# A decoder block on one core: the second composed weight by seven block products, the first one's scaling on ScalarE

## The chip, the core and the metric

The kernel runs on one core of a Trainium2 chip. The metric is the device time of one execution in microseconds, the median of several runs. The engines are named as in the profile: PE is TensorE's matrix multiply and PEld its weight load, DVE is VectorE, ACT is ScalarE, POOL is GpSimd, SP is SyncE, which only issues DMAs. All data are f32, and an f32 matmul leaves two records in the trace.

## What is computed

`x` is (8, 256, 256): 8 sequences of 256 tokens with 256 features. Three blocks follow one another, each with a residual and a layer norm behind it.

- Four layers of attention (8 heads of 32; four local ones with a causal window of 128, four linear ones over buckets of 64), each followed by an MLP 256 to 1024 to 256 with exact gelu.
- A cross attention to a context of 120 tokens.
- A feed-forward block whose two weights are first composed:

```python
def _compose_weight(logits, A, B):        # A (64, d_in, 64), B (64, 64, d_out)
    vals, idx = top_k(logits, 32)
    w = softmax(vals)
    return einsum('k,kir,kro->io', w, A[idx], B[idx])
W1 = _compose_weight(fc1_logits, fc1_A, fc1_B)   # 256 x 1024
W2 = _compose_weight(fc2_logits, fc2_A, fc2_B)   # 1024 x 256
h = gelu(x @ W1);  y = h @ W2
```

The change lies in the composition. Each weight is a sum of 32 weighted products of rank 64. Two of them side by side have rank 128, which is one pass of TensorE's rows; so there are 16 pairs per weight.

## The kernel before, in words

**Order.** Lines 1100 to 1109 put PE, ACT, DVE and POOL under a manual schedule: each engine runs its instructions in the order in which the Python code calls them. The main loop (L1173) has 32 steps, one per layer and sequence. A step runs the attention of one sequence split in pieces (`old`, `new`, `after` are three sequences at different points), an MLP four steps behind (`ff`), and a piece of the composition. A second loop (L1283) does the cross attention and the feed-forward block.

**The composition.** The 16 pairs of a weight are taken in 8 groups of `PG` = 2; `n` is 0 for the first weight and 1 for the second, `g` the group. A group passes through these stages, each a method:

- `Group.__init__` (L325): six indirect DMAs from POOL's queue (L302), four for the rows of A (`ga`) and two for the rows of B (`gbt`).
- `weigh` (L341): VectorE multiplies the A rows by their softmax weights (L350), four instructions per group, 128x128 each for n = 0 and 128x512 for n = 1.
- `turns` (L359): TensorE transposes the weighted A (L369), VectorE and ScalarE copy it from PSUM to `at` (L372 for n = 0, L377 and L379 for n = 1).
- `block(i)`, i from 0 to 3 (L382): TensorE multiplies `at` and the B rows into one PSUM bank; VectorE adds the bank to the running sum in `w2c` (L420 for the first group, L422 after; for n = 0 the last group goes to `w1c`, L400). For n = 0 a block is two matmuls of 512 columns (L387), for n = 1 four of 256 columns (L410).

`Compose.run` (L448) ties the stages together: `weigh` of the next group if that has not been done, the four blocks of the current group, `gather` of the group after the next, `turns` of the next. It is called three times in step 1, twice in steps 2 and 3, and once in each of steps 4 to 12 (L1184, L1221, L1247); the second weight's blocks run in steps 5 to 12. In steps with an MLP, `weigh` is called earlier (L1219). `filled` is true as long as the composition has not ended.

**Around it in a step.** Before `run` at L1247 stand: `new.exps` (L670: exponentials L672 and L673, then L685 for heads 0 and 1), `ff.second(1)` (matmuls L561 into the bank `ps_p`), `after.turn` (transposes L213 of the next sequence, evicted by VectorE at L222 and ScalarE at L223), the exponentials of heads 2 and 3, and `softmax_q` (L696 to L700). After `run` stand `totals` and `divide` (L709 to L715), `nxt_m.centre` (L195, and two bias adds on POOL, L230), `ff.second(0)` (L561, then the add L234 that empties `ps_p`), and the next step's `after.moments` (L181 to L189), `new.qkv` (L602, L622, evicted at L611 and L629 to L642), `linear_sums`, `divide_c` (L751 to L757), `turn_p` (L767, copies L770 and L772), `turn_sums` (L490 to L493 on POOL) and `scores` (L653).

**PSUM.** Two pools of four banks: `bank_s` for scores and projections, `bank_g` for the rest, the composition among it. `ps_p` holds one of the four from `second(1)` to `second(0)`.

**Seven products elsewhere.** The MLP's first matmul already goes by seven block products in place of eight (`first_sums` L472, class `Seven` L482, `one` L509 with its matmuls at L512): sums of blocks are formed on POOL (L476 to L479, 128x512, and L490 to L493, 128x128), and each product is four matmuls of 128 columns.

Of the kernel before, what the change touches and what calls it, by code (L numbers as in the profile page):

```python
# [8 lines left out]
F32 = mybir.dt.float32  # L9
I32 = mybir.dt.int32  # L10
AF = mybir.ActivationFunctionType
ALU = mybir.AluOpType
# [3 lines left out]
P = 128  # L16
# [5 lines left out]
def tile_decoder_postln(  # L22
# [46 lines left out]
    NP, _, R = fc1_A.shape  # L69
    TOPK = 32  # L70
    NPAIR = TOPK // 2
# [51 lines left out]
    w1c = const.tile([P, NC, FF], F32, name="w1c")  # L123
    w2c = const.tile([P, NF, D], F32, name="w2c")
# [46 lines left out]
    def bank_g(name):  # L171
        return ps_g.tile([P, 512], F32, tag="bank_g", name=name)
# [34 lines left out]
    def turn(src, tag, name, gain=None, shift=None):  # L207

        dst = work.tile([P, NC, T], F32, tag=tag, name=f"xT_{name}")
        ps = bank_g(f"ps_t_{name}")  # L210
        for c in range(NC):
            for i in range(WT):
                nc.tensor.transpose(  # L213
                    ps[:, c * T + i * P : c * T + (i + 1) * P],
                    src[:, i, c * P : (c + 1) * P],
                    ident,
                )
        if gain is None:
# [3 lines left out]
        nc.vector.tensor_scalar(dst[:, 0, :], ps[:, :T], gain(0), shift(0), ALU.mult, ALU.add)  # L222
# [29 lines left out]
    comp = comp_stack.enter_context(tc.tile_pool(name="comp", bufs=1))  # L252
# [59 lines left out]
    PG = 2  # L312
# [11 lines left out]
    class Group:  # L324
# [16 lines left out]
        def weigh(self):  # L341

            n, g, n_c = self.n, self.g, tables[self.n][2]
            wts = tops[n][2]
            self.aw = []
            for k, a in enumerate(self.a):
                t = g * PG + k
                aw = comp.tile([P, n_c, 2, R], F32, tag="aw", name=f"aw{n}_{t}", bufs=2)
                for e in range(2):
                    nc.vector.tensor_scalar(  # L350
                        aw[:, :, e, :],
                        a[:, e, :].rearrange("p (c r) -> p c r", c=n_c),
                        wts[:, 2 * t + e : 2 * t + e + 1],
                        None,
                        ALU.mult,
                    )
                self.aw.append(aw.rearrange("p c e r -> p c (e r)"))

        def turns(self):  # L359
            n, n_c = self.n, tables[self.n][2]  # L360
            self.at = []
            for k, aw in enumerate(self.aw):
                name = f"{n}_{self.g}_{k}"
                at_ = comp.tile([P, n_c * P], F32, tag="at", name=f"at{name}", bufs=4)
                for q in range(0, n_c, 4):
                    ps = bank_g(f"ps_at{name}_{q}")
                    m = min(4, n_c)
                    for c in range(m):
                        nc.tensor.transpose(ps[:, c * P : (c + 1) * P], aw[:, q + c, :], ident)  # L369
# [12 lines left out]
        def block(self, i):  # L382
            ps = bank_g(f"ps_w{self.n}_{self.g}_{i}")
            if self.n == 0:
                m, n = divmod(i, 2)
                for k in range(PG):
                    nc.tensor.matmul(  # L387
                        ps,
                        self.at[k][:, m * P : (m + 1) * P],
                        self.b[k][:, n * 512 : (n + 1) * 512],  # L390
                        start=k == 0,
                        stop=k == PG - 1,
                    )

                dst = w2c.rearrange("p f d -> p (f d)").rearrange("p (m o) -> p m o", m=NC)
                dst = dst[:, m, n * 512 : (n + 1) * 512]
                src = ps
                if self.g == NPAIR // PG - 1:
                    final = w1c[:, m, :].rearrange("q (j p) -> q p j", j=NF)
                    nc.vector.tensor_add(  # L400
                        final[:, n * 64 : (n + 1) * 64, :],
                        dst.rearrange("q (p j) -> q p j", j=NF),
                        src.rearrange("q (p j) -> q p j", j=NF),
                    )
                    return
            else:
                for e in range(2):
                    j = 2 * i + e
                    for k in range(PG):
                        nc.tensor.matmul(  # L410
                            ps[:, e * D : (e + 1) * D],
                            self.at[k][:, j * P : (j + 1) * P],
                            self.b[k],
                            start=k == 0,
                            stop=k == PG - 1,
                        )
                dst = w2c[:, 2 * i : 2 * i + 2, :].rearrange("p j d -> p (j d)")
                src = ps
            if self.g == 0:
                nc.vector.tensor_copy(dst, src)  # L420
            else:
                nc.vector.tensor_add(dst, dst, src)  # L422

    class Compose:

# [17 lines left out]
        def turn(self):  # L443
            self.turned, self.weighed = self.weighed, None
            if self.turned:
                self.turned.turns()

        def run(self):  # L448
            if self.turned is None:
                return  # L450
            if not self.weighed:
                self.weigh()
            for i in range(4):
                self.turned.block(i)
            self.gather()
            self.turn()

# [24 lines left out]
    class Seven:  # L482
# [26 lines left out]
        def one(self, n, ps, start=False, stop=False):  # L509

            for f in range(4):
                nc.tensor.matmul(  # L512
                    ps[:, f * P : (f + 1) * P],
                    self.ws[n][:, f * P : (f + 1) * P],
                    self.rhs[n],
                    start=start and f == 0,
                    stop=stop and f == 3,
                    skip_group_check=True,
                )
# [50 lines left out]
    class Attention:  # L570
# [99 lines left out]
        def exps(self):  # L670
            name = self.name
            nc.scalar.activation(self.qs, self.qs, AF.Exp)  # L672
            nc.scalar.activation(self.ke, self.ke, AF.Exp)  # L673
            self.p = []

            self.psum = small.tile([P, HL, 3], F32, tag="psum", name=f"psum_{name}")
            self.head_exps(range(2))

        def head_exps(self, heads):
            for h in heads:  # L680
# [173 lines left out]
    class Composed(Seven):  # L854
# [21 lines left out]
        def turn(self):  # L876
            self.xT = turn(xs[self.b], "xTm", self.name)
# [14 lines left out]
    class Context:  # L892
# [222 lines left out]
    new = Attention(0)  # L1115
    first = {n: top_k(n) for n in range(2)}
# [43 lines left out]
    compose.gather()  # L1160
    new.scores()
    new.exps()
    new.head_exps((2, 3))
    new.softmax_q()
    new.totals()
    new.divide(range(HL))
# [1 line left out]
    old, new = new, after  # L1168
# [4 lines left out]
    for s in range(1, UNITS + 1):  # L1173
# [3 lines left out]
        filled = cross is None  # L1177
# [55 lines left out]
        if turn_cx:  # L1233
            i = 2 * (s - (UNITS - B + LAG))
            cx.turn(i)
            cx.take()
        if new:
            new.exps()
        if ff:
            ff.second(1)  # L1240
        if after:
            after.turn()
        if new:
            new.head_exps((2, 3))
            new.softmax_q()
        if filled:
            compose.run()  # L1247
# [31 lines left out]
        old, new = new, after  # L1279
# [109 lines left out]
```

## Time and profile before

| | |
|---|---|
| median of 3 runs | 1248.43 us (1246.93 to 1251.41) |
| the profiled execution | 1256.8 us, its span 1254.9 us |
| mean granted clock of TensorE | 0.99 |
| from one group of the second weight to the next | 34.8 to 35.0 us |

Busy time in us, by stage of the span:

| stage | span | PE | DVE | ACT | POOL |
|---|---|---|---|---|---|
| 0 to 157 us, start and first weight | 157.0 | 132.8 | 113.0 | 48.3 | 78.2 |
| 157 to 192 us, last group of the first weight | 34.9 | 34.6 | 26.1 | 18.1 | 11.8 |
| 192 to 443 us, the second weight's eight groups | 250.9 | 250.9 | 177.2 | 133.0 | 85.4 |
| 443 us to the end | 812.1 | 803.7 | 531.5 | 429.3 | 207.3 |

In a row of the timeline stand the start, the time from first start to last end, the engine, the line, the operation, output and inputs, the shape and the number of instructions; in brackets the idle time before it and the instruction that ended it. Rows of one line without a gap are merged. A matmul's end is modelled, so pace is read from starts.

### The profile page before, as it was taken

To read this page: it belongs to the slowest core of one execution; us is meant where nothing else is said; L and a number is where in the kernel's file an instruction comes from. 1 tells how busy PE (TensorE), PEld (TensorE's weight loads), DVE (VectorE), ACT (ScalarE), POOL (GpSimd) and SP (SyncE) were. 2 spreads that over 40 slices of the span, in tenths; PEclk is the share of its full clock that TensorE was granted. 3 is DMA by queue.
4 is the path that set the end of the run, shared out by engine and by line. 5 is a ranking of instruction groups with operands and counts; after the bars stand their busy time and mean duration, and the time that the engine had idled before them with its cause. 6 is when DMAs were issued, how large, how long until landed. Compare 5 with 4: busy or idle time off the path is not lost.

```text
span 1254.9 us, 23452 instructions
## 1 busy us (share of the span) xinstructions
PE 1222.0 (97%) x8905; PEld 969.1 (77%) x8905; DVE 847.8 (68%) x2435; ACT 628.7 (50%) x1738; POOL 382.7 (31%) x596
## 2 busy tenths in 40 slices
PE   5999999999999999999999999999999999999998
PEld 3555678888888888888878888788888777777787
DVE  5787877767767667777777776777765454556543
ACT  2222544555555556667766677566773334233322
POOL 5445433333334111222322221242213323222210
PEclk8998999999999999999999999999999999999999
DMA  4532212111120021002001000120000000000000
GB/s 131 168 91 83 81 51 81 43 43 43 65 73 20 1 84 39 2 2 72 1 1 39 2 1 17 57 69 1 26 10 10 9 9 9 18 17 9 9 14 22
DMA packets 29502, 47.77 MB, mean 38 GB/s; under 512 B 3150, under 2 KB 22734, under 8 KB 29134
## 3 DMA queue, kind: packets, MB, share of 16 engines
q0 software_dynamic: 6656, 20.98, 5.6%
q10 hardware_dynamic: 13024, 14.07, 3.4%
q1 hardware_dynamic: 9710, 11.23, 2.8%
q8 instruction: 70, 1.15, 0.4%
q14 instruction: 42, 0.34, 0.1%
HBM read 44.17 MB, written 2.10 MB: 37 GB/s over the span
## 4 chain that ended last, share of the span: by engine, by line
PE 92%; DVE 3%; ACT 2%; POOL 1%; issue 1%; another core or an unknown queue 0%; DMA 0%; POOLq 0%; ACTq 0%; DVEq 0%
PE ps_p_m L561 17%; PE qkv_a L622 8%; PE ps_h_m_u L512 7%; PE ps_h_m_a L512 5%; PE ps_w L387 4%; PE ps_w L410 4%; PE ps_h_m_d L512 4%; PE ps_p_a L240 4%; PE ps_qk_a L602 4%; PE ps_p_f L561 4%; PE ps_pT_a L767 3%; PE sc_a L653 3%; PE ps_y_c L1085 2%; PE ps_xq_c L996 2%; PE ps_xk_c L996 2%; PE ps_xv_c L996 2%
## 5 line engine op out<-in xcount | busy, mean ns | idle before, releaser
L561 PE MATMUL ps_p_m<-w,h_m 128*128 128x256 f32 x1024 | 231.5, 379 | 0.0
L561 PEld LDWEIGHTS ps_p_m<-w,h_m 128*128 128x128 f32 x1024 | 189.8, 190 | 23.5 <-ACT h_m L827 0.3
L622 PE MATMUL qkv_a<-wa,xT_a 128*128 128x512 f32 x256 | 115.7, 595 | 0.0
L230 POOL TENSOR_TENSOR x<-x,b 128x256 f32<-128x256 f32 x64 | 48.2, 773 | 209.5 <-DVE xn_m L195 209.4
L685 ACT ACTIVATE p_a<-sc_a,nm_a 128x128 f32<-128x128 f32 (+1 forms) x256 | 103.9, 426 | 1.9 <-DVE nm_a L666 1.7
L622 PEld LDWEIGHTS qkv_a<-wa,xT_a 128*128 128x128 f32 x256 | 49.1, 192 | 48.1 <-issue 46.3
L230 POOL TENSOR_TENSOR x<-x,bo 128x256 f32<-128x256 f32 x64 | 48.2, 772 | 118.4 <-DVE xn_a L195 113.6
L666 DVE TENSOR_REDUCE nm_a<-sc_a 128x1 f32<-128x128 f32 (+1 forms) x256 | 79.7, 353 | 4.4
L827 ACT ACTIVATE h_m<-h_m,cols 128x128 f32<-128x128 f32 x256 | 78.6, 405 | 6.2 <-DVE h_m L549 5.5
L512 PE MATMUL ps_h_m_a<-xT_m,w 128*128 128x128 f32 x512 | 71.4, 283 | 0.0
L302 POOL DMA_INDIRECT ga<-in_L_ffn_fc_A_dram,idx_a x64 | 62.1, 971 | 21.2 <-issue 16.6
L512 PE MATMUL ps_h_m_u<-tx_m,w 128*128 128x128 f32 x512 | 67.6, 275 | 0.0
L629 ACT COPY v<-qkv_a 128x256 f32<-128x256 f32 x64 | 23.8, 372 | 86.3 <-PE qkv_a L622 85.0
L602 PE MATMUL ps_qk_a<-xT_a,wa 128*128 128x256 f32 x256 | 64.0, 395 | 2.8 <-DVE nm_a L666 2.1
L512 PEld LDWEIGHTS ps_h_m_a<-xT_m,w 128*128 128x128 f32 x512 | 63.2, 194 | 4.2 <-issue 1.6
L240 PE MATMUL ps_p_a<-wo,oT_a 128*128 128x256 f32 x256 | 65.4, 380 | 0.0
L662 DVE TENSOR_TENSOR sc_a<-sc_a,causal 128x256 f32<-128x256 f32 x128 | 54.5, 425 | 15.5 <-PE sc_a L653 15.5
L715 DVE TENSOR_TENSOR p_a<-p_a,psum_a 128x384 f32<-128x384 f32 x128 | 62.9, 553 | 1.1
L512 PEld LDWEIGHTS ps_h_m_u<-tx_m,w 128*128 128x128 f32 x512 | 62.3, 192 | 0.0
L602 PEld LDWEIGHTS ps_qk_a<-xT_a,wa 128*128 128x128 f32 x256 | 50.4, 199 | 11.1 <-ACT p_a L685 2.8
L561 PE MATMUL ps_p_f<-w2c,h_f 128*128 128x256 f32 x256 | 57.8, 379 | 0.0
L767 PE MATMUL ps_pT_a<-ident,p_a 128*128 128x128 f32 x384 | 52.3, 278 | 5.6 <-ACT pT_a L772 5.0
(245 smaller groups left out, 2655.2 us busy)
## 6 DMA issues: line engine op xcount, KB each, us to landing
w<-in_L_attn_W_dram ACTq DMA_DIRECT2D x8, 1024.0 KB, 7.6
xwkv<-in_L_xattn_Wkv_dram SPq DMA_DIRECT2D x1, 2048.0 KB
x_c<-in_x_dram SPq DMA_DIRECT2D x8, 256.0 KB, 2.7
out_dram<-y_f SPq DMA_DIRECT2D x16, 128.0 KB, 1.7
x<-in_x_dram ACTq DMA_DIRECT2D x6, 256.0 KB, 2.7
ga<-in_L_ffn_fc_A_dram,idx_a POOLq DMA_INDIRECT x64
xwq<-in_L_xattn_Wq_dram SPq DMA_DIRECT2D x1, 1024.0 KB
xwo<-in_L_xattn_Wout_dram SPq DMA_DIRECT2D x1, 1024.0 KB
```

The costliest lines, as they stand in the source:

```text
L230: nc.gpsimd.tensor_add(xb[:, i, :], xb[:, i, :], bias)
L240: nc.tensor.matmul(ps[:, i * D : (i + 1) * D], lhs(c, i), w[:, c, :], start=c == 0, stop=c == n_in - 1,)
L512: nc.tensor.matmul(ps[:, f * P : (f + 1) * P], self.ws[n][:, f * P : (f + 1) * P], self.rhs[n], start=start and f == 0, stop=stop and f == ...
L561: nc.tensor.matmul(self.ps[:, i * D : (i + 1) * D], self.h[k][:, f, :], self.w2[:, half * 4 + f, :], start=k in (11, 22) and f == 0, stop= ...
L602: nc.tensor.matmul(ps[:, s * T : (s + 1) * T], wa[:, c, s * HW : (s + 1) * HW], xT[:, c, :], start=c == 0, stop=c == NC - 1,)
L622: nc.tensor.matmul(t, xT[:, c, w * P : (w + 1) * P], wa[:, c, 2 * HW :], start=c == 0, stop=c == NC - 1,)
L666: nc.vector.tensor_reduce(self.nmax[:, h, w : w + 1], sc[:, s], AX.X, ALU.max, negate=True)
L685: nc.scalar.activation(flat[:, s], sc[:, s], AF.Exp, bias=self.nmax[:, h, w : w + 1], accum_out=self.psum[:, h, w : w + 1],)
L715: nc.vector.tensor_tensor(p, p, self.psum[:, h, :, None].to_broadcast([P, 3, P]), ALU.mult)
L767: nc.tensor.transpose(pp[:, k * P : (k + 1) * P], p[:, k, :], ident)
L827: nc.scalar.activation(dst[:, f, :], src[:, f * P : (f + 1) * P], AF.Gelu, bias=col("ff", i))
L996: nc.tensor.matmul(ps[:S2], lhs(c), w[:, c, off : off + 512], start=c == 0, stop=c == NC - 1)
```

## The change

For the second weight (n = 1) a group's 1024 x 128 by 128 x 256 products, two of them summed, are seen as a 2 x 2 block product: the blocks of A are two halves of `at` (512 columns) by the two pairs, those of B the two pairs by two halves of 128 columns. Eight block products become seven. `combine` forms eight sums on POOL, four of 128x128 and four of 128x512, two of them in place; it is called behind `turns`. `seven` makes the products on four banks and adds them to five running sums on VectorE: the four quarters of `w2c` and a tile `u` that three of the quarters share; after the last group POOL adds `u` to those three. Further: `weigh` for n = 0 goes to ScalarE, `at` has two buffers for four, and while the composition lasts all four head exponentials stand behind `after.turn` (the first two stood before it). `block` serves only n = 0 now, with the same instructions.

```diff
                 for e in range(2):
-                    nc.vector.tensor_scalar(
...
+                    if n == 0:
+                        nc.scalar.mul(dst, src, w)
+                    else:
+                        nc.vector.tensor_scalar(dst, src, w, None, ALU.mult)
...
-                at_ = comp.tile([P, n_c * P], F32, tag="at", name=f"at{name}", bufs=4)
+                at_ = comp.tile([P, n_c * P], F32, tag="at", name=f"at{name}", bufs=2)
...
-                for e in range(2):
-                    j = 2 * i + e
-                    for k in range(PG):
-                        nc.tensor.matmul(
-                            ps[:, e * D : (e + 1) * D],
-                            self.at[k][:, j * P : (j + 1) * P],
-                            self.b[k],
-                            start=k == 0,
-                            stop=k == PG - 1,
-                        )
-                dst = w2c[:, 2 * i : 2 * i + 2, :].rearrange("p j d -> p (j d)")
...
+        def combine(self):
+
+            a = [[at_[:, m * 512 : (m + 1) * 512] for at_ in self.at] for m in range(2)]
+            b = [[b_[:, n * P : (n + 1) * P] for n in range(2)] for b_ in self.b]
+            name = f"{self.n}_{self.g}"
+            s1, s2, s4 = (
+                comp.tile([P, 512], F32, tag=f"cs{i}", name=f"cs{i}_{name}") for i in (1, 2, 4)
+            )
+            t1, t2, t4 = (
+                comp.tile([P, P], F32, tag=tag, name=f"ct_{tag}_{name}") for tag in ("lb", "pb", "t4")
+            )
+            nc.gpsimd.tensor_sub(t1, b[0][1], b[0][0])
+            nc.gpsimd.tensor_sub(t2, b[1][1], t1)
+            nc.gpsimd.tensor_sub(t4, b[1][0], t2)
+            nc.gpsimd.tensor_sub(b[0][1], b[1][1], b[0][1])
+            nc.gpsimd.tensor_add(s1, a[1][0], a[1][1])
+            nc.gpsimd.tensor_sub(s2, s1, a[0][0])
+            nc.gpsimd.tensor_sub(s4, a[0][1], s2)
+            nc.gpsimd.tensor_sub(a[1][0], a[0][0], a[1][0])
+            self.factors = {
+                1: (a[0][0], b[0][0]),
+                2: (a[0][1], b[1][0]),
+                3: (s4, b[1][1]),
+                4: (a[1][1], t4),
+                5: (s1, t1),
+                6: (s2, t2),
+                7: (a[1][0], b[0][1]),
+            }
+
+        def one(self, i, ps, start=False, stop=False):
+            a, b = self.factors[i]
+            for f in range(4):
+                nc.tensor.matmul(
+                    ps[:, f * P : (f + 1) * P],
+                    a[:, f * P : (f + 1) * P],
+                    b,
+                    start=start and f == 0,
+                    stop=stop and f == 3,
+                    skip_group_check=True,
+                )
+
+        def seven(self):
+            c = [[w2c[:, 4 * m : 4 * m + 4, n * P : (n + 1) * P] for n in range(2)] for m in range(2)]
+            u = comp.tile([P, 4, P], F32, name="csum_u") if self.g == 0 else Group.u
+            Group.u = u
+
+            def take(dst, ps, first=False):
+                src = ps.rearrange("p (f i) -> p f i", f=4)
+                if self.g == 0 and first:
+                    nc.vector.tensor_copy(dst, src)
+                else:
+                    nc.vector.tensor_add(dst, dst, src)
+
+            name = f"ps_w{self.n}_{self.g}"
+            p6 = bank_g(f"{name}_6")
+            self.one(6, p6, True, True)
+            take(u, p6, True)
+            p12 = bank_g(f"{name}_12")
+            self.one(1, p12, start=True)
+            take(u, p12)
+            p53 = bank_g(f"{name}_53")
+            self.one(5, p53, start=True)
+            take(c[1][1], p53, True)
+            p74 = bank_g(f"{name}_74")
+            self.one(7, p74, start=True)
+            take(c[1][1], p74)
+            self.one(2, p12, stop=True)
+            take(c[0][0], p12, True)
+            self.one(3, p53, stop=True)
+            take(c[0][1], p53, True)
+            self.one(4, p74, stop=True)
+            take(c[1][0], p74, True)
+            if self.g == NPAIR // PG - 1:
+                for m, n in ((0, 1), (1, 0), (1, 1)):
+                    nc.gpsimd.tensor_add(c[m][n], c[m][n], u)
...
             if self.turned:
                 self.turned.turns()
+                if self.turned.n:
+                    self.turned.combine()
...
             self.psum = small.tile([P, HL, 3], F32, tag="psum", name=f"psum_{name}")
-            self.head_exps(range(2))
...
     new.exps()
-    new.head_exps((2, 3))
+    new.head_exps(range(HL))
...
         if new:
             new.exps()
+            if not filled:
+                new.head_exps((0, 1))
...
         if new:
-            new.head_exps((2, 3))
+            new.head_exps((2, 3) if not filled else range(HL))
             new.softmax_q()
```

More of the change, by code (lines that the diff above doesn't have):

```diff
@@ L349, in weigh @@
                 for e in range(2):
[L350 to L355, printed above, removed]
-                    )
+                    dst = aw[:, :, e, :]
+                    src = a[:, e, :].rearrange("p (c r) -> p c r", c=n_c)
+                    w = wts[:, 2 * t + e : 2 * t + e + 1]
+                    if n == 0:
+                        nc.scalar.mul(dst, src, w)
+                    else:
+                        nc.vector.tensor_scalar(dst, src, w, None, ALU.mult)
                 self.aw.append(aw.rearrange("p c e r -> p c (e r)"))
@@ L383, in block @@
             ps = bank_g(f"ps_w{self.n}_{self.g}_{i}")
-            if self.n == 0:
-                m, n = divmod(i, 2)
-                for k in range(PG):
-                    nc.tensor.matmul(
-                        ps,
-                        self.at[k][:, m * P : (m + 1) * P],
-                        self.b[k][:, n * 512 : (n + 1) * 512],
-                        start=k == 0,
-                        stop=k == PG - 1,
[L393 to L405, printed above, removed]
-            else:
-                for e in range(2):
-                    j = 2 * i + e
-                    for k in range(PG):
-                        nc.tensor.matmul(
-                            ps[:, e * D : (e + 1) * D],
-                            self.at[k][:, j * P : (j + 1) * P],
-                            self.b[k],
-                            start=k == 0,
-                            stop=k == PG - 1,
-                        )
-                dst = w2c[:, 2 * i : 2 * i + 2, :].rearrange("p j d -> p (j d)")
-                src = ps
@@ L419, in block @@
-            if self.g == 0:
-                nc.vector.tensor_copy(dst, src)
-            else:
-                nc.vector.tensor_add(dst, dst, src)
+            m, n = divmod(i, 2)
+            for k in range(PG):
+                nc.tensor.matmul(
+                    ps,
+                    self.at[k][:, m * P : (m + 1) * P],
+                    self.b[k][:, n * 512 : (n + 1) * 512],
+                    start=k == 0,
+                    stop=k == PG - 1,
+                )
+            dst = w2c.rearrange("p f d -> p (f d)").rearrange("p (m o) -> p m o", m=NC)
@@ new lines, in block @@
+            dst = dst[:, m, n * 512 : (n + 1) * 512]
+            if self.g == NPAIR // PG - 1:
+                final = w1c[:, m, :].rearrange("q (j p) -> q p j", j=NF)
+                nc.vector.tensor_add(
+                    final[:, n * 64 : (n + 1) * 64, :],
+                    dst.rearrange("q (p j) -> q p j", j=NF),
+                    ps.rearrange("q (p j) -> q p j", j=NF),
+                )
+            elif self.g == 0:
+                nc.vector.tensor_copy(dst, ps)
+            else:
+                nc.vector.tensor_add(dst, dst, ps)
@@ new lines, in combine @@
+        def combine(self):
[7 more added lines that the diff above has]
+                comp.tile([P, P], F32, tag=tag, name=f"ct_{tag}_{name}") for tag in ("lb", "pb", "t4")
+            )
+            nc.gpsimd.tensor_sub(t1, b[0][1], b[0][0])
[15 more added lines that the diff above has]
+            }
@@ new lines, in one @@
+        def one(self, i, ps, start=False, stop=False):
+            a, b = self.factors[i]
+            for f in range(4):
+                nc.tensor.matmul(
+                    ps[:, f * P : (f + 1) * P],
[4 more added lines that the diff above has]
+                    skip_group_check=True,
+                )
+        def seven(self):
[27 more added lines that the diff above has]
+            take(c[1][0], p74, True)
+            if self.g == NPAIR // PG - 1:
+                for m, n in ((0, 1), (1, 0), (1, 1)):
+                    nc.gpsimd.tensor_add(c[m][n], c[m][n], u)
@@ L424, in tile_decoder_postln, with blocks @@
+        def blocks(self):
+            if self.n:
+                self.seven()
+            else:
+                for i in range(4):
+                    self.block(i)
     class Compose:
@@ L452, in run @@
                 self.weigh()
-            for i in range(4):
-                self.turned.block(i)
+            self.turned.blocks()
             self.gather()
```

## The prediction

> **What bounds the kernel.** I read the page first (busy shares, then the chain), then busy time by stage, then the timeline of one step engine by engine.
>
> ```profile
> span 1254.9 us, 23452 instructions
> PE 1222.0 (97%) x8905; PEld 969.1 (77%) x8905; DVE 847.8 (68%) x2435; ACT 628.7 (50%) x1738; POOL 382.7 (31%) x596
> PE 92%; DVE 3%; ACT 2%; POOL 1%; issue 1%; another core or an unknown queue 0%; DMA 0%; POOLq 0%; ACTq 0%; DVEq 0%
> ```
> ```profile
> 0.00:157.04 157.04, 132.78 (x790) 81.89 (x791) 112.98 (x341) 48.27 (x154) 78.23 (x105) 0.93 0.35 111
> ...
> 191.89:442.80 250.91, 250.91 (x1925) 210.13 (x1924) 177.20 (x480) 132.96 (x383) 85.39 (x117) 1.00 0.16 46
> ```
> TensorE is the bound: 92% of the chain. The stage rows (span, then busy PE, PEld, DVE, ACT, POOL, then clock) say more. From 191.9 to 442.8 us, from the second weight's first group to its eighth (34.8 to 35.0 us apart), TensorE has no idle time at all: an instruction saved there is time saved, and any wait put on it is time lost. In the first 157 us, where the first weight is composed, it idles 24 us and the clock is 0.93; work moved there counts only if it stands in one of those waits.
>
> One such step, TensorE's view of a group and of two of the seven block products that the MLP already uses (L512):
>
> ```profile
> 217.52 1.05 PE L512 MATMUL ps_h_m_d<-tx_m,s 128*128 128x128 f32 x8
> 218.41 1.06 PE L512 MATMUL ps_h_m_a<-xT_m,w 128*128 128x128 f32 x8
> ...
> 226.74 7.07 PE L410 MATMUL ps_w<-gbt,at 128*128 128x256 f32 x32
> 233.65 2.20 PE L369 MATMUL ps_at<-ident,aw 128*128 128x128 f32 x16
> ```
> Starts are to be read, not durations (ends are modelled), and an f32 matmul leaves two records.
>
> **1. The products, removed and added.** A group takes 233.65 - 226.74 = 6.91 us for 16 matmuls of 256 columns, 0.432 each. A block product of four matmuls of 128 columns takes 218.41 - 217.52 = 0.89. The new group has seven products, 28 matmuls: 7 x 0.89 = 6.23. So 0.68 us less per group, and with 8 groups **-5.4 us**. Counting multiplications (7 for 8) would promise 0.86; the shorter matmul costs 0.22 and not half of 0.432.
>
> **2. VectorE's evictions.** Per group four adds from PSUM (L422, 0.69 each) become seven: +2.1 us of VectorE.
>
> ```profile
> 228.42 0.42 DVE L700 TENSOR_TENSOR qs_a<-qs_a,qsum_a 128x256 f32<-128x256 f32 x1
> 228.76 0.68 DVE L422 TENSOR_TENSOR w2c<-w2c,ps_w 128x512 f32<-128x512 f32 x1
> 230.40 0.69 DVE L422 TENSOR_TENSOR w2c<-w2c,ps_w 128x512 f32<-128x512 f32 x1 [0.95 <-PE ps_w L410]
> ```
> Three of the four waited 0.95 to 1.04 us for TensorE, 3.0 together; the 2.1 fit in there, and after the last product one add remains, as now. What can show is the banks. `bank_g` has four; one is held by the MLP's `ps_p`, one by the transposed input until ScalarE's L223. The move of the head exponentials puts L223 first (ready about 228.1), so the third product (wanted at 228.5) finds it free. The fourth (wanted at 226.74 + 3 x 0.89 = 229.41) needs the first add done: start 228.8, end 229.5, so 0.1 late: 8 x 0.1 = **+0.8**. Products 2, 3, 4 re-enter banks read 0.3 us or more before. In the step at 401 us the first add comes 0.7 later (403.68 after a start of 400.98, against 2.02) because L700 took 0.81 there: **+0.6**.
>
> **3. GpSimd's sums.** Eight new instructions per group. Prices: L490 to L493 (128x128, same operation) 0.45 long, 0.42 apart; L476 to L479 (128x512) 1.27 to 1.44, the four in 5.4 us. Together 1.7 + 5.4 = 7.1 us, in GpSimd's queue between the gathers of `run` and L230's bias of the next MLP, L189 and L490 of the next step.
>
> ```profile
> 233.65 0.94 POOL L302 DMA_INDIRECT gbt<-in_L_ffn_fc_B_dram,idx_b  x1 [4.70 <-PE ps_w L410]
> ...
> 248.05 0.45 POOL L490 TENSOR_TENSOR tx_m<-xT_m 128x128 f32<-128x128 f32 x1 [5.93 <-DVE xT_m L222]
> ```
> Two waits hold them: the gather waits 4.70 for the matmuls that read the old B rows, and L490 waits 5.93. With the new order the first B tile is last read by product 7, the fourth in line, so that gather can start near 230.6 and not 233.65; three more at 1.25 end about 235.5, the sums about 242.7 to 244.5, the rest of the queue before 247. The sums are wanted 30 us later. By itself this costs nothing; without that cover 7.1 - 5.9 would delay L490, and TensorE after 1.4 us more. The last group has three adds of 1.3 instead, with no gathers left; what they cost VectorE lies within the waits of part 4.
>
> **4. What the sums do to VectorE.** The same add, L700, stands in the trace twice:
>
> ```profile
> 402.06 1.42 POOL L477 TENSOR_TENSOR s<-s,w 128x512 f32<-128x512 f32 x1
> 402.95 0.81 DVE L700 TENSOR_TENSOR qs_a<-qs_a,qsum_a 128x256 f32<-128x256 f32 x1
> ```
> 0.42 alone (fence above), 0.81 beside a GpSimd sum, ending 0.28 after it: it stood still until GpSimd was done. Four scalings of L350 take 0.87 alone and 3.35 under L476 and L477 (94.78 us), while L422, one operand in PSUM, keeps its 0.69. So VectorE's instructions with all operands in SBUF are exposed. From 235.3 on (before's times less 0.68) these are L709, four L715, two L195 and L184, later L754 and L757. Walked through with a start of 235.5: L715 meets the small sums and waits three times about 0.27; one L195 meets the first large one, 1.0; L184 another, 0.8; together 2.6. VectorE has waits to lose before it matters: 0.24 + 0.17 (L234, L611), 1.28 and 0.70 (L634), 2.4 together.
>
> ```profile
> 243.19 0.29 DVE L634 TENSOR_REDUCE qm_a<-qkv_a 128x4 f32<-128x128 f32 x1 [1.28 <-ACT v L629]
> 244.91 0.29 DVE L634 TENSOR_REDUCE qm_a<-qkv_a 128x4 f32<-128x128 f32 x1 [0.70 <-ACT v L629]
> 246.90 0.55 DVE L770 COPY pT_a<-ps_pT_a 128x384 f32<-128x384 f32 x1
> ```
> After that there is no slack: L770 ends at 247.45, and the third head's scores (L653, begun at 247.10) go on at 247.50 in the bank that it empties. So each us beyond 2.4 is a us of TensorE. The remainder is 0.1 to 0.2 at a start of 235.5, up to 0.9 for a start of 237 to 238.5 (then L754 and L757 meet the large sums and L230), 1.1 at worst, 0 at best. I take 0.1, by the start that I can derive: 8 x 0.1 = **+0.8**, ends 0 and +8.8.
>
> The Trainium skill (SBUF — State Buffer, Who interferes with whom) says that VectorE instructions with two SBUF inputs, or in a two-port mode, share an exclusive port pair with GpSimd, and that whoever starts second blocks until the other is done. It speaks against this change. The rows agree for L700 and L350; no row shows the tiny L754 (0.17 in all 32) blocked, which by the page's rule would be. By the page every exposed instruction pays; by the rows only those above the slack do.
>
> **5. The first weight's scaling on ScalarE.** 32 instructions of 128x128 leave VectorE (0.20 to 1.3 each) for ScalarE; no row shows this form there, the nearest are L827 (128x128 from SBUF, 0.31 apart, 0.41 long) and L672 (0.42 for 256 columns). I take 0.31, top 0.42. In six of the groups ScalarE waits 4.4 to 7.9 us before its copy of the transposes (L372), so it is hidden, and VectorE's regained time is not on the path either: its L422 there waits for TensorE. Not so the first group:
>
> ```profile
> 22.75 1.01 DVE L350 TENSOR_SCALAR aw<-ga,wts 128x128 f32<-128x128 f32 x4
> 23.37 1.13 PE L369 MATMUL ps_at<-ident,aw 128*128 128x128 f32 x4 [1.12 <-DVE aw L350]
> ```
> TensorE waits for the scaling here. ScalarE is in L223 until 23.43, so its four end at 24.05 (first pair) and 24.7, the transposes about 25.3 and not 24.45; scores, exponentials and L602 stand behind. **+0.8**, ends +0.4 (the half clock ends at 31.4 whatever is queued) and +2.5 (one half-clock window of 3.4 us more). In the third step the four heads and the scaling now end about 133.0, where the transposes want them at 132.45: **+0.3**.
>
> **6. At nothing:** `at` with two buffers (its writers already stand behind the matmuls that read the old ones on TensorE), the later head exponentials elsewhere (their banks are wanted at 239, freed by 231.5).
>
> **Sum:** -5.4 + 0.8 + 0.6 + 0.8 + 0.8 + 0.3 = -2.1 us, against the profiled execution's 1256.8 (span 1254.9 and 1.9 around it). The runs' median is 8.4 lower; I move the difference over: 1248.4 - 2.1 = **1246.3**. About 0.3% (3.7 us) is what a measurement of this kernel can tell from no change.
>
> **Rivals.**
> *A, GpSimd's sums hold up VectorE (slower).* One mechanism, in the 10 us before the scores. Without the 0.8 of part 4 the sum is -2.9; with c us per step it is -2.9 + 8c: break-even at 0.36, slower than 0.3% from 0.83; at c = 1.1 it gives 1254.3. For it: L700's 0.81 and no slack behind L770. Against it: 2.4 us of waits ahead, and 0.17 in all of L754.
> *B, the early stage gains.* TensorE waits 2.8 us for VectorE's L267 at 76.7 and loses 3.4 us in half-clock windows at 110 to 116.7. If VectorE's relief removes one of them: -2.1 - 3.4 = 1242.9. Against it: VectorE's run before 76.7 starts at an eviction that waited for TensorE.
> *C, the change does not do what it says:* four adds chained on few banks make each of the products 7, 2, 3, 4 wait 0.17, and the 0.68 is gone: -2.1 + 5.4 = 1251.7.
>
> **Chances.** Forecast 0.52 (own range 1243 to 1249; 0.22 of it faster, 0.30 the same), A 0.22 (0.16 slower, 0.06 same), B 0.16 (0.15 faster), C 0.10 (0.06 slower, 0.04 same). Faster 0.37, same 0.41, slower 0.22. Range 1241.0 to 1254.5: B and most of A.
>
> **What would show it.** Product starts 0.89 apart and the group 6.2 to 6.4 long (1, 2). A first B gather near 3.9 us after the group's start (3). L715, L195, L184 longer than 0.55, 0.41, 0.17, and L770 no later after the transposes than now (4). Steps of 34.2 to 34.4 us between the second weight's groups; scores at about 25.3 in the start (5). I am wrong if those steps are 34.8 or more, or if the first 157 us shift by more than 2 us.

## The result, and the profile after

The changed kernel takes 1254.14 us, the median of 18 runs (1252.76 to 1256.8); the kernel before, measured beside it, takes 1248.93 (18 runs, 1246.79 to 1253.48). The ratio is 1.0038, with a 95% interval of 1.0027 to 1.0048. The change costs some 5 us; a small gain was forecast.

Lines of the code behind the diff have moved: L410 is L445 now, L422 is L464, L715 is L787, L653 is L726, L770 is L842.

From the page of the changed kernel, its span, its busy shares and its chain:

```profile
span 1251.4 us, 23991 instructions
PE 1220.4 (98%) x9097; PEld 972.6 (78%) x9097; DVE 880.0 (70%) x2427; ACT 639.7 (51%) x1770; POOL 446.2 (36%) x663
PE 84%; DVE 12%; ACT 2%; POOL 1%; issue 1%; DMA 0%; POOLq 0%; ACTq 0%; DVEq 0%
```

TensorE's busy time fell by 1.6 us, but VectorE's share of the chain went from 3% to 12%: a new wait. The two spans themselves must not be subtracted. The execution profiled before was 8 us longer than the median of its kernel. A second profile of the same kernel on another chip (e1 below), whose median is 1259, agrees with it within 0.4 us at every matmul, and the changed kernel on that other chip (e5 below) is 8.3 us later at 157 us than it is here. So the 8 us go with the chip: they lie before 157 us, in stretches like the 1.56 us that TensorE waits for "issue" at 46.2 us. Behind that point the two traces can be compared instruction by instruction.

The stage of the second weight, from the start of its first group to the end of its eighth, in the busy time by stage (stage, span, then PE, PEld, DVE, ACT, POOL):

```profile
185.25:437.53 252.28, 249.21 (x2117) 212.99 (x2115) 214.35 (x504) 133.85 (x383) 137.20 (x173) 1.00 0.16 46
```

It was 250.91 long with PE busy for all of it; it is 252.28 now and PE idles for 3.1. TensorE's starts give the account:

| in this stage | us |
|---|---|
| 8 groups, 6.43 us long and not 6.91 (226.64 - 220.21) | -3.84 |
| the fourth product in the step at 398 us, behind VectorE's late first add | +0.6 |
| six steps, 0.55 each, at the scores | +3.3 |
| the last step (no gathers in it), at the transposes and the scores | +1.3 |
| sum, against a measured 252.28 - 250.91 = 1.37 | +1.36 |

One step earlier, where the first large sums run (158.8 to 165.1 us), another 1.39 is lost in the same way. Here is the place in a middle step. VectorE, then GpSimd, then TensorE, each from its own timeline of the changed kernel:

```profile
229.38 2.81 DVE L787 TENSOR_TENSOR p_a<-p_a,psum_a 128x384 f32<-128x384 f32 x4
232.12 2.72 DVE L195 TENSOR_SCALAR xn_m<-x,mv_m,rs_m 128x256 f32<-128x256 f32 x2
...
235.36 0.41 DVE L181 BATCH_NORM_STATS2 st_a<-x 128x6 f32<-128x256 f32 x1
235.81 0.18 DVE L182 BATCH_NORM_AGGREGATE mv_a<-st_a 128x2 f32<-128x6 f32 x1
...
236.55 0.74 DVE L184 TENSOR_SCALAR rs_a<-mv_a 128x2 f32<-128x2 f32 x1
...
240.43 0.55 DVE L842 COPY pT_a<-ps_pT_a 128x384 f32<-128x384 f32 x1
```
```profile
231.01 0.77 POOL L427 TENSOR_TENSOR gbt<-gbt,gbt 128x128 f32<-128x128 f32 x1
231.74 1.60 POOL L428 TENSOR_TENSOR cs<-at,at 128x512 f32<-128x512 f32 x1
233.42 1.26 POOL L429 TENSOR_TENSOR cs<-cs,at 128x512 f32<-128x512 f32 x1
234.76 1.28 POOL L430 TENSOR_TENSOR cs<-at,cs 128x512 f32<-128x512 f32 x1
235.99 1.27 POOL L431 TENSOR_TENSOR at<-at 128x512 f32<-128x512 f32 x1
```
```profile
240.09 0.69 PE L726 MATMUL sc_a<-qk_a 32*128 32x128 f32 x6
241.04 0.92 PE L726 MATMUL sc_a<-qk_a 32*128 32x128 f32 x10 [0.26 <-DVE pT_a L842]
```

The same three before, in the step from 226.74 us:

```profile
236.35 1.97 DVE L715 TENSOR_TENSOR p_a<-p_a,psum_a 128x384 f32<-128x384 f32 x4
238.24 0.86 DVE L195 TENSOR_SCALAR xn_m<-x,mv_m,rs_m 128x256 f32<-128x256 f32 x2
...
241.15 0.17 DVE L184 TENSOR_SCALAR rs_a<-mv_a 128x2 f32<-128x2 f32 x1
```

Four L787 took 1.97 before, two L195 0.86, L184 0.17. They are 0.84, 1.86 and 0.57 longer, 3.27 in all, and each stands under a GpSimd sum. L181 and L182 also read and write SBUF alone; they kept 0.41 and 0.18 under L430. From 236 on VectorE has no bracket, so no wait of its own left; L842, which empties the bank that the third head's scores need, starts 0.55 late against the transposes, and TensorE stops in the middle of the scores.

Outside these stages two half-clock stretches differ. In the start and near 945 us, the stage rows of the changed kernel (the 1.00 behind the busy times of the row above is the granted clock):

```profile
31.40:34.80 3.40, 3.40 (x7) 1.95 (x6) 3.26 (x10) 0.94 (x5) 0.00 (x0) 0.51 0.58 196
942.80:946.20 3.40, 3.40 (x32) 3.31 (x35) 0.84 (x5) 0.07 (x1) 3.20 (x7) 0.50 0.00 0
```

Before, the first stretch ended at 31.4 us (10.24 long and not 13.65), and the second lasted 3.41 us (from 949.6) and not 6.83 (from 942.7). The difference costs 1.27 and 1.58 us in this trace. Neither is shown to be the change's: in e5, the same kernel again, both stretches are as long as before. With the start's own 0.82 the whole account is 0.82 + 1.27 + 1.39 + 1.37 + 1.58 = 6.4 us, against 5.2 measured (3.4 to 6.0 by the interval); without the two stretches it is 3.6. The early part has no trace of before on the same chip, so what lies between stays open.

### The profile page after: what moved, and what is told of

The parts are those of the page before. It is cut to its first block, busy times and chain, and to the rows that moved or that the text cites. A ratio compares the mean times of both kernels' runs of the same rounds, so it can differ in the third digit from the quotient of the medians.

```text
span 1251.4 us, 23991 instructions
## 1 busy us (share of the span) xinstructions
PE 1220.4 (98%) x9097; PEld 972.6 (78%) x9097; DVE 880.0 (70%) x2427; ACT 639.7 (51%) x1770; POOL 446.2 (36%) x663
## 4 chain that ended last, share of the span: by engine, by line
PE 84%; DVE 12%; ACT 2%; POOL 1%; issue 1%; DMA 0%; POOLq 0%; ACTq 0%; DVEq 0%
PE ps_p_m L634 14%; PE ps_h_m_u L585 7%; PE qkv_a L695 6%; PE ps_h_m_a L585 5%; PE ps_w L387 4%; PE ps_h_m_d L585 4%; PE ps_p_a L240 4%; PE ps_w L445 4%; PE ps_p_f L634 4%; PE ps_qk_a L675 3%; PE sc_a L726 3%; DVE p_a L787 3%; PE ps_pT_a L839 2%; PE ps_y_c L1157 2%; PE ps_xq_c L1068 2%; PE ps_xk_c L1068 2%
## 5 line engine op out<-in xcount | busy, mean ns | idle before, releaser
L230 POOL TENSOR_TENSOR x<-x,b 128x256 f32<-128x256 f32 x64 | 47.8, 767 | 186.2 <-DVE xn_m L195 186.2
L230 POOL TENSOR_TENSOR x<-x,bo 128x256 f32<-128x256 f32 x64 | 48.2, 772 | 112.8 <-DVE xn_a L195 107.8
L787 DVE TENSOR_TENSOR p_a<-p_a,psum_a 128x384 f32<-128x384 f32 x128 | 76.4, 657 | 1.1
L735 DVE TENSOR_TENSOR sc_a<-sc_a,causal 128x256 f32<-128x256 f32 x128 | 54.5, 425 | 14.6 <-PE sc_a L726 14.6
L387 PE MATMUL ps_w<-gbt,at 128*128 128x512 f32 x128 | 56.6, 595 | 0.0
```

Source lines behind the costliest of these rows:

```text
L230: nc.gpsimd.tensor_add(xb[:, i, :], xb[:, i, :], bias)
L387: nc.tensor.matmul(ps, self.at[k][:, m * P : (m + 1) * P], self.b[k][:, n * 512 : (n + 1) * 512], start=k == 0, stop=k == PG - 1,)
L787: nc.vector.tensor_tensor(p, p, self.psum[:, h, :, None].to_broadcast([P, 3, P]), ALU.mult)
```

## The experiments

Theory 1: GpSimd's sums hold up VectorE's instructions with SBUF operands, L787, L195 and L184, and the copies behind them reach TensorE late. Theory 2: the seven products pay by themselves, through banks and evictions. Theory 3: the weighing on ScalarE makes the start late.

e1 to e8 ran on a chip whose kernel before takes 1258 to 1259 us, e9 to e11 on one with 1260, e12 on one with 1250; so ratios are compared, each with the kernel before on its own chip.

### e1: the kernel before, again

> The kernel before, unchanged, for a second profile of it: the one shown lasted 1256.8 us where the median of its runs is 1248.9, and its trace holds some 8 us of stalls and half-clock stretches before 157 us that the changed kernel's trace does not. Expected 1249, with the steps between groups of the second weight 34.85 us apart as before, and the first group of the first weight at about 35 us. If the half-clock stretches belong to the kernel, they come again at the same places; if they are a matter of one execution, they do not.

1259.11 us, ratio 0.9998 (0.9985 to 1.0012). The steps are 34.85 us apart, and the half-clock stretches come again at the same places (after 21, 48, 110 and 950 us). They and the early waits belong to this kernel on such a chip.

### e2: no sums

```diff
-            s1, s2, s4 = (
...
-            nc.gpsimd.tensor_sub(t1, b[0][1], b[0][0])
...
-            nc.gpsimd.tensor_sub(a[1][0], a[0][0], a[1][0])
+            s1, s2, s4 = a[1][0], a[0][1], a[0][0]
+            t1, t2, t4 = b[0][1], b[1][0], b[1][1]
```

> The changed kernel without the eight sums on GpSimd: every product takes plain blocks of the two factors, so the second composed weight is not the reference's; everything else (seven products, five running sums, the weighing on ScalarE) stays. Theory 1 (GpSimd's sums hold up VectorE's L787, L195 and L184, and so the transposes and scores behind them): the losses that the trace shows in the steps with such sums, 0.9 + 1.4 + 6 x 0.55 + 1.3 = 6.9 us, go, and the time is 1247.3. Theory 2 (the seven products pay by themselves: banks that come free late, more evictions on VectorE): the time stays at 1253 to 1254. Theory 3 (the loss is the late start, the weighing on ScalarE): 1253 to 1254 as well.

1255.8 us against 1258.6, ratio 0.9972 (0.9952 to 0.9991). VectorE in a middle step of this kernel (L775 is L787 of the changed one):

```profile
238.65 1.97 DVE L775 TENSOR_TENSOR p_a<-p_a,psum_a 128x384 f32<-128x384 f32 x4
240.53 0.73 DVE L195 TENSOR_SCALAR xn_m<-x,mv_m,rs_m 128x256 f32<-128x256 f32 x2
```

Their old lengths are back, TensorE waits nowhere at the scores, the group takes 6.43 us (7.02 in the step at 400 us, as in the changed kernel), and the steps are 34.38 us apart and not 34.85: what the group saves, the step saves. Against e1's trace it gains 3.2 us from the second weight on and loses 1.1 at the start. Theory 2 falls: the products earn what they save. The time expected was for the first chip; here the ratio is to be read. Of the 6.9 us expected, 0.9 (a difference near 143 us) turned out to be one of chips and not of kernels: e1 and e5, both kernels on such a chip, differ by 0.1 us from 113 to 176 us.

### e3: the weighing alone

```diff
-                    nc.vector.tensor_scalar(
...
+                    if n == 0:
+                        nc.scalar.mul(dst, src, w)
+                    else:
+                        nc.vector.tensor_scalar(dst, src, w, None, ALU.mult)
```

> The kernel before with one part of the change alone: the first weight's groups are weighed on ScalarE. Theory 1: the first group comes 0.8 us later (ScalarE weighs after its half of the transposed rows, VectorE did it at once), the later groups are hidden; 1249.7. Theory 3 (the weighing carries the loss, and the slow clock seen after the start, 1.3 us, belongs to the later start): 1251 to 1254, with the first group near 37.1 us instead of 35.0.

Ratio 1.0003 (0.9991 to 1.0015). The first group comes 0.55 us later than in e1's trace and the end 0.59 later. Theory 3 falls as the main cause.

### e4: the sums a step later, the large ones ahead of the weighing

```diff
             ff.turn_sums()
+            compose.sum_b()
...
+            compose.sum_a()
             old.out(0)
```

`sum_b` issues the four sums of 128x128, `sum_a` those of 128x512.

> The changed kernel with the same eight sums emitted one step later: the four of 128x128 behind the turned sums of the MLP rows, the four of 128x512 behind the centring of the next attention's rows, where the trace shows GpSimd idle and VectorE mostly at work on PSUM. Theory 1, with the addition that only VectorE's SBUF operations (L787, L195, L184, L356) wait for GpSimd while those with PSUM operands do not: the 0.55 to 1.4 us per step go and at most 1 us per step comes back at the weighing L356; 1247 to 1250. Theory 2 or 3: 1253 to 1255. If every VectorE operation waits for GpSimd: 1254 or more.

1270.21 us, ratio 1.0086 (1.006 to 1.0112): worse, and theory 1 missed it. That every VectorE operation waits (1254 or more) would cover the time, but not the trace: under these sums VectorE's L234, with an operand in PSUM, keeps its 0.69. VectorE's timeline shows one cause:

```profile
226.88 3.56 DVE L356 TENSOR_SCALAR aw<-ga,wts 128x512 f32<-128x512 f32 x4
```

L787 keeps 1.97 here, but the second weight's weighing L356, with all operands in SBUF, takes 3.56 where it took 1.67. The first eviction of the products starts 2.6 us behind the group's start and not 2.0, the fourth product waits for a bank (0.29), and the group takes 7.05 us. In all steps but the first and the last, copies of the transposes were 1 to 2.6 us late on top; most steps are 35.1 us apart, three are 35.8 to 37.2. The lengthening of L356 is theory 1's mechanism, at a place with still less slack; the late copies are no part of it (see e5).

### e5: the changed kernel, again

> The changed kernel, unchanged, beside the others of this call: its first trace and that of the kernel before came from executions that differ by 8 us of stalls ahead of 157 us, so the step lengths are to be read again. Every theory expects a ratio of 1.004 to the kernel before. Theory 1 expects the stages of 4 to 12 of its trace to show again 0.55 us of waits for the transposed head's copy per middle step, and 1.3 to 1.4 in the second and the last.

1271.76 us, ratio 1.012 (1.0096 to 1.0143): 14 us, not 5. So the cost depends on the chip. Its trace loses 1.4 us in the first step with sums, 1.3 to 3.9 in each middle step (the two longest, 3.9 and 3.5, hold a half-clock stretch of 3.41 us each), 1.3 in the last. VectorE in a middle step (group start 231.06):

```profile
240.19 0.69 DVE L377 COPY at<-ps_at 128x512 f32<-128x512 f32 x1 [1.22 <-PE ps_at L369]
...
241.29 4.47 DVE L787 TENSOR_TENSOR p_a<-p_a,psum_a 128x384 f32<-128x384 f32 x4
245.68 2.65 DVE L195 TENSOR_SCALAR xn_m<-x,mv_m,rs_m 128x256 f32<-128x256 f32 x2
```

The copy L377 begins 1.1 us after the end of the transposes it reads (in the first trace 0.04); ScalarE's L379 begins 1.0 late. L787 then starts 10.2 us behind the group's start and not 9.2, and meets the long sums and not the short ones: 4.47. The same late copies stand in e2, which has no sums, so the sums don't cause them; there they cost nothing. e1 and e3, on the same chip with the order of before, have none (0.04 to 0.21 from the second weight's first group on). Within e5 the step whose copies were late least (from 305.57 us: 0.28, 0.43 and 1.28) lost least, 1.3.

### e6: only the small sums

```diff
-            s1, s2, s4 = (
...
+            s1, s2, s4 = a[1][0], a[0][1], a[0][0]
...
-            nc.gpsimd.tensor_add(s1, a[1][0], a[1][1])
-            nc.gpsimd.tensor_sub(s2, s1, a[0][0])
-            nc.gpsimd.tensor_sub(s4, a[0][1], s2)
-            nc.gpsimd.tensor_sub(a[1][0], a[0][0], a[1][0])
```

> The changed kernel with only the four 128x128 sums on GpSimd; the four of 128x512 are left out and plain blocks stand for them, so the second composed weight is not the reference's. Theory 1: the small sums hold up L787 by under 1 us per step, which the 2.4 us of slack ahead of the third head's copy take; the time is that with no sums at all (ratio 0.997 to the kernel before, measured), 0.996 to 0.998. If the number of sums and not their length is what costs: half of the loss stays, 1.000 to 1.001.

1253.74 us, ratio 0.9973 (0.9963 to 0.9982), as with no sums. L787 takes 1.97 to 2.54, within the slack. The four long sums carry the loss; the four short ones alone, where they were, cost nothing.

### e7, e8: the long sums in two pairs, and with vector weighing

```diff
             ff.turn_sums()
+            compose.sum_b()
...
+            compose.sum_a()
             old.out(0)
```

`sum_b` issues two of the four sums of 128x512 here, `sum_a` the other two; those of 128x128 stay where they were. e8 has vector weighing besides, as before the change.

> The changed kernel with the four 128x512 sums moved away in pairs, the 128x128 ones where they were: two behind the turned sums of the MLP rows, where VectorE works on the scores in PSUM for 2.9 us, two behind the centring of the next attention's rows, where it works on PSUM for 2.8 us and the weighing L356 follows. The run with all four large sums in front of L356 lengthened L356 from 1.67 to 3.56 us, the evictions behind it started late, and the group took 7.05 us instead of 6.43. Theory 1, narrowed to that (VectorE's operations with SBUF operands alone wait for GpSimd, those with PSUM operands do not): L356 and L787 both keep their length, the group takes 6.4, the steps are 34.4 apart, and the time is that with no sums: ratio 0.996 to 0.998. If operations on PSUM wait as well: the scores' steps L735 and L739 lengthen and the ratio is 1.002 or more.

> The same, with the first weight's groups weighed on VectorE again as in the kernel before (part of the change undone). Alone on the kernel before, the weighing on ScalarE moved the work from 60 us on by 0.5 to 0.6 us. Theory 1: 0.5 us under the run with split sums, ratio 0.996 to 0.997, the fastest version here. If ScalarE's weighing had spared VectorE something in the first steps: no faster, or slower.

Ratios 1.0044 (1.0029 to 1.006) and 1.0046 (1.0033 to 1.006). On VectorE theory 1 holds as narrowed: L787 1.96 to 2.55, L195 0.73, L356 1.67, the statistics on PSUM unchanged, the group 6.5 us. But a wait of another kind took the gain. TensorE in e7:

```profile
256.11 0.70 PE L240 MATMUL ps_p_a<-wo,oT_a 128*128 128x256 f32 x2 [0.58 <-POOL oT_a L895]
```

The output projection waits for a 128x64 memset that stands behind the two sums in GpSimd's queue; each of eight steps lost 0.84. Vector weighing alone moved nothing that these intervals can tell.

### e9, e10: behind the memset; the small sums ahead of the gathers

```diff
-            compose.sum_b()
...
         old.values()
+        if ff:
+            compose.sum_b()
```

`old.values` issues the memset. e10 adds the edit shown under e12. Both keep e8's vector weighing.

> The split sums with vector weighing, and one step more: the pair of 128x512 sums that stood ahead of the attention's 128x64 memset of oT_a on GpSimd is emitted behind it. In the trace of the split sums L787, L195, L184 and L356 kept their lengths (so the sums no longer hold VectorE up), the group took 6.49 us, but the output projection L240 waited 0.58 us for that memset and each step lost 0.84. Theory 1: that wait goes, seven to eight steps gain 0.8 each, and the ratio to the kernel before is 1.0046 - 7.5 x 0.84 / 1258 = 0.9996 or, with the half-clock stretch of 3.4 us near 950 left aside, 0.998. If the sums under the scores' statistics cost something that the trace did not name: 1.002 or more.

> The same with the four 128x128 sums emitted ahead of the next group's gathers: they then run beside the products and not under L787, and the gathers are issued 3 us later. Theory 1: another few tenths per step off VectorE that have cover already, so 0.997 to 0.9995, no slower than the run with the gathers first. If the later gathers bring the weighing L356 to a wait for data: slower, 1.002 or more, with a wait for a DMA ahead of L356.

1255.17 us against 1259.77, ratio 0.9962 (0.9944 to 0.9981), and 1256.57, ratio 0.997 (0.9958 to 0.9983). Both are faster than the kernel before, by 0.4 and 0.3%, on a chip where the late copies occur (e9 has them, 1.1 to 1.9 us; in e10, whose gathers are issued later, they are gone). Two of VectorE's rows and one stage row of e9:

```profile
238.82 1.97 DVE L806 TENSOR_TENSOR p_a<-p_a,psum_a 128x384 f32<-128x384 f32 x4
240.70 0.73 DVE L195 TENSOR_SCALAR xn_m<-x,mv_m,rs_m 128x256 f32<-128x256 f32 x2
```
```profile
225.00:260.00 35.00, 34.99 (x298) 29.95 (x297) 27.29 (x73) 19.05 (x56) 18.83 (x25) 1.00 0.14 39
```

PE is busy for 34.99 of 35.00 us again, steps are 34.44 apart: the same eight sums, and their 7 us of GpSimd per step cost less than 0.1 us (34.38 in e2, without sums). Both weigh on VectorE, which by e7 and e8 makes no difference that can be told. Neither ran on a chip like the first.

### e11: the gathers last

```diff
             self.turned.blocks()
-            self.gather()
             self.turn()
+            self.gather()
```

> The changed kernel with only the order on GpSimd turned round: all eight sums first, then the three gathers of the next group. On this chip the steps with gathers lost 2.1 to 2.6 us each and the copies L377 and L379 began 1.0 to 1.9 us after the transposes they read, where the first trace of the changed kernel shows 0.04 to 0.2; the last step, which has no gathers, shows 0.04 and lost 0.7 to 1.3. Theory A (the gathers' data, landing at the time of the copies, delay them, and L787 then meets the long sums): with the gathers behind the sums the lag falls to 0.04 to 0.2 in every step, each step loses 1.3 to 1.4 as the last one does, and the ratio is 1.004 to 1.007. Theory B (the lag comes from the products or from the sums themselves): the lag stays at 1.0 to 1.9, ratio 1.010 or more.

1305.5 us, ratio 1.0358 (1.0338 to 1.0378). The lag of L377 and L379 fell to 0.04 to 0.2, as theory A has it, but the steps with gathers lost 5.5 to 7.5 us, and the last, without, 1.3: neither theory has both. L787 takes 5.2 in every step, as the sums now begin right at the copies. The late starts moved to ScalarE's next copies:

```profile
262.82 0.37 ACT L816 COPY qsT_a<-ps_q_a 128x256 f32<-128x256 f32 x1 [3.72 <-remote]
```

The bracket names no engine of the core; the matmuls that it reads had begun 3.7 us before. The gathers' data were moving from 258.5 to 266. In this step TensorE waits 4.1 us at the transposes; most of the rest goes to a half-clock stretch behind the wait (262.2 to 269.05 us, granted clock 0.50; the scores take 1.77 us there for 1.32). Seven steps of e11 have one; of the other runs only e5 has any in the second weight's steps. So the late copies follow the gathers in time. What holds them up is not shown.

### e12: the small sums first

```diff
             self.turned.blocks()
+            if self.weighed and self.weighed.n:
+                self.weighed.combine_b()
             self.gather()
```

> The changed kernel with one thing moved: the four 128x128 sums stand ahead of the next group's gathers, the four of 128x512 stay behind them. The gathers are then issued some 3 us later, and the run with the small sums early showed no late copies with that. Theory A (on this chip the late copies L377 and L379, 1.0 to 1.9 us, push L787 into the long sums, and that is why the changed kernel loses 17 us here and 5 on the first chip): the lag is gone, L787 keeps near 2.0 us for four, and only what comes behind it, L195, L184 and the small operations before the copy of the transposed head, meets the long sums; 0.5 to 1.1 us per step, ratio 1.002 to 1.006. Theory B (the long sums cost the same wherever they fall before the scores): 2 to 3 us per step as before, ratio 1.010 or more.

1253.88 us against 1249.67, ratio 1.004 (1.0027 to 1.0053). It ran on a chip like the first, where no copy is late in the changed kernel either, so it tells nothing of the lag. It does tell of place. In the middle steps L787 keeps 1.97 and L195 0.86, yet each loses 0.8, 0.25 more than in the changed kernel. VectorE, just ahead of the copy of the third head (L848):

```profile
239.64 1.05 DVE L835 TENSOR_TENSOR cn_a<-cs_a,rk_a 128x96 f32<-128x96 f32 x1
```

An instruction of 0.26 us waits 0.79 for one sum, with no slack behind it. One wait there costs more than 3.3 us of waits earlier.

## Why the prediction was wrong, point by point

1. *Products, -0.68 per group.* Measured -0.48, in e2 as well. The pace of 0.89 was right (220.21, 221.10, 221.99); the rest stands in point 2.
2. *Banks +0.1 per group, and +0.6 at 401 us.* About 0.2 went from the third product to the sixth (222.96 - 221.99 is 0.97, and the next two take 1.89), where banks are used again; that each of these is a wait for a bank is argued, not shown. So 0.48 is left where 0.58 was forecast. The 0.6 came as predicted, 0.51 of it as TensorE's wait for `csum_u`.
3. *Sums hidden on GpSimd.* The first B gather came 4.2 us after the group's start (forecast 3.9), the sums ran from 8.9 to 17.0 us behind it (8.8 to between 16.0 and 17.8). That they cost GpSimd nothing is right. That earlier gathers cost nothing holds for the first chip alone.
4. *VectorE, +0.1 per step.* **This step failed.** The mechanism, the instructions and the start were right; the waits were mis-sized, and the slack a little. I had three of L715 lose 0.27, one L195 lose 1.0 and L184 0.8, together 2.6 against 2.4. Measured are 0.84, 1.86 and 0.57, together 3.27: both L195 pay, because between two sums that stand back to back VectorE gets one instruction through and then waits for the next. Against them stand 2.7 of slack and not 2.4: VectorE's instructions overlap by 0.07 to 0.09 us where they don't wait (before, L234 starts 0.24 behind the end of L195; now 0.08 ahead of it), and four waits went. So the remainder over the slack is 0.55, not 0.1. And I took eight like steps: in the first and the last no gathers stand ahead of the sums, which begin right at the copies; there L787 takes 5.2 us in the last (1.97 before), and 1.39 and 1.3 are lost. Together 6.0 us where the sum had 0.8. A difference of two near numbers, 2.6 and 2.4, was the whole term; the ends 0 and 8.8 held it.
5. *Start +0.8.* Transposes at 24.05 and scores at 25.25, as forecast, 0.82 late. The half-clock stretch did not end at 31.4 us whatever was queued: it was 3.4 us longer, 1.27 more. 2.09 lies within the ends given, in part by luck, as e5 has the shorter stretch with the same kernel. In e3 the weighing alone costs 0.5. The 0.3 of the third step can't be told from the traces.
6. *At nothing:* nothing in the traces speaks against it.

The premise of point 4, that every VectorE instruction with all operands in SBUF is exposed, was too wide. Two rows just ahead of the L700 that I read showed it: under the same L477 (402.06 to 403.47 us) these kept the lengths that they have at 227.74 and 228.18.

```profile
402.26 0.41 DVE L698 TENSOR_REDUCE qsum_a<-qs_a 128x8 f32<-128x256 f32 x1
402.71 0.20 DVE L699 RECIPROCAL qsum_a<-qsum_a 128x8 f32<-128x8 f32 x1
```

The walk of point 4 priced none of that kind, so this cost it nothing. The tiny L754, which no row had shown blocked, can be: as L826 of the changed kernel it took 0.67 us for 0.17 beside L230 at 133.0 us.

Rival A was the case. Its line, -2.9 + 8c with slower from c = 0.83, has c = 6.0 / 8 = 0.75 here and gives +3.1; with the 0.8 that points 1 and 2 lack it is 3.9, within the interval of 3.4 to 6.0. What fills it up to the measured 5.2 is not shown; the half-clock stretch in the start (1.27) would, but it changes from trace to trace. Rival C (products that wait) is excluded by e2, rival B by e5, whose first 176 us end within 0.1 of e1's. Of the signals, "L770 no later after the transposes than now" and "34.8 or more" decided: steps are 34.9 apart.

## What to carry to other kernels

Where work is put on GpSimd that reads SBUF, walk VectorE's instructions beside it. Let each tensor_tensor with both inputs in SBUF, and each tensor_scalar with SBUF operands alone, wait for a whole GpSimd instruction, one for one. In these runs whatever had an operand in PSUM kept its length, and so did the batch-norm pair, the reduction and the reciprocals. If the sum of those waits comes near the slack, take it as not hidden, and look for another place in the step; in e9 the same sums cost less than 0.1 us per step. When moving work in a queue, look at the smallest instruction behind it and who waits for that (e7's memset).

## What the runs showed of the hardware that was not expected

- The wait is paired and mutual: under L787, and under the first L195 of a middle step, the 128x512 sums themselves stretch from 1.27 to between 1.46 and 1.60 us. VectorE's L464, L234 and L735, with an operand in PSUM, kept 0.69, 0.68 and 0.43. Of the small ones L184 (128x2) took 0.74 for 0.17 and L835 of e12 1.05 for 0.26, while the reciprocal just ahead of L835 (L833, 128x3) kept 0.18 under the same sum.
- On the two chips of 1258 us and more, ScalarE's and VectorE's copies of transposes began 1.0 to 1.9 us late in most steps (up to 2.6 in e4) while the gathers' data moved, with the same program that shows 0.04 to 0.2 on the first chip; with the order of before (e1, e3) they did not. There the changed kernel costs 1.2% and not 0.4%. That the late copies make the difference is read from e5's trace; e11 and e12, meant to test it, could not. Moving the gathers 3 us (e10) removed the lag on a chip where e9 has it; the cause is open.
- Half-clock stretches last 3.4 us or a multiple (3.41, 6.83, 10.24, 13.65). The one near 945 us is 6.83 long in the changed kernel's first trace and 3.41 in e5, the same kernel: 1.6 us of time that no edit made.
